# Mask steps, norm scalars and the accumulator's transpose in a four-layer graph network: what goes to VectorE, and in which order

## The chip, the cores and the metric

The kernel runs on one core of a Trainium2 chip. A core has TensorE (PE, matrix products into PSUM), VectorE (DVE), ScalarE (ACT), GpSimd (POOL), SyncE (SP, which issues most DMAs here) and 16 DMA engines. Each engine works through its own queue in order; they wait for one another by semaphores. The metric is the device time of one execution in microseconds. Instructions of the profile are named by line of the kernel before (L557), engine, and what they write and read (e<-s,mask_add).

## The reference

Sixteen graphs of 1024 nodes with 128 features share one 0/1 adjacency matrix. Three attention layers and one last layer are applied in turn:

```
for l in 0..2:                                   # 8 heads of 16
    Q, K, V = x @ Wq, x @ Wk, x @ Wv
    attn = softmax(where(adj == 0, -inf, Q K^T / 4))
    x = layer_norm(x + (attn @ V) @ Wo + bo) * ln1_g + ln1_b
    x = layer_norm(x + relu(x @ W1 + b1) @ W2 + b2) * ln2_g + ln2_b
h = x @ W; e = leaky_relu(h @ a_src [:, None] + h @ a_dst [None, :], 0.2)
y = softmax(where(adj == 0, -inf, e)) @ h + x
out = layer_norm(y) * ln_gamma + ln_beta
layer_norm(z) = (z - mean) * (var + 1e-5) ** -0.5
```

## The kernel before

The fast path treats 48 **blocks**, one for each pair of image and attention layer, in groups of four images: four blocks of layer 0, four of layer 1, four of layer 2. A block has 32 **steps** (2 groups of heads, 2 halves of the queries, 8 tiles of keys); `now[0]` counts the steps of the whole program, and `now[0] % 32` is the step's place in its block. A step (`score_step`, L537 on) computes two score pairs `s` of 128 keys by 1024 (L545), each in one of three PSUM tiles, and makes masked exponentials `e` of them:

- In a **single** step the first pair goes through ScalarE's exponential (L553) and is then multiplied by the 0/1 mask on GpSimd (L554). The second pair gets a large negative number added where the mask forbids it, on VectorE (L557), and ScalarE's exponential afterwards (L569).
- In a **double** step (`BOTH_ON_DVE`, L41) both pairs go through VectorE's addition and ScalarE's exponential after it; GpSimd does nothing. ScalarE has two exponentials in either case. The exponentials behind an addition are issued a pair late, so that ScalarE doesn't stand waiting for VectorE.

Four steps later (`AHEAD`) `av_step` multiplies the values with the exponentials into the one accumulator `acc` (L574). After 8 such products `finish` transposes it on VectorE (`tt`, L585), inverts the sums (L588) and has GpSimd scale it (`A`, L589); this happens at steps 3, 11, 19 and 27 of a block, and the next half's first product may not start before the transpose has read `acc`.

Between the steps `piece()` puts small tasks of other blocks, by tables of due steps (`AT`): the projections of the next block (values at 5 and 7, keys at 9 and 11, queries at 17 and 19, with VectorE's `lo` at L473 or L477), the previous block's output projection at 13 and 15, the first FFN product at 23, 25, 27 and 29, and the second at 31 and 35 (step 3 of the next block). Output projection and second FFN product end in `add_and_stats`: VectorE adds the residual (L420), takes four statistics (L413) and four aggregates (L415), which leave mean and variance in `mv`. `scalars` on GpSimd then negates the mean (L433), adds epsilon to the variance (L434) and raises it to -1/2 (L435); `subtract_scale` applies both (L441). The first norm of a block does this in two halves of four columns, the second in one of eight. When the last layer of an image is due, its tasks (`last_tasks`: edges at L774, `aggregate` at L779 to L792) run between the steps of other images' blocks.

The order on PE, ACT and SP is the order of the code (`manual_schedule`). On DVE and POOL a scheduler sets the order by priority and modelled readiness: `soon()` raises the priority, and `tc.issue_after(ins)` keeps what follows behind `ins` on that engine. `low[n]` is the subtraction of `lo` traced in step n; a mask addition and a transpose of step n + 2 are kept behind it. `behind["dve"]` is the last mask addition traced.

Of the kernel before, what the change touches and what calls it, by code (L numbers as in the profile page):

```python
# [15 lines left out]
OP = mybir.AluOpType  # L16
# [8 lines left out]
EPS = 1e-5  # L25
# [12 lines left out]
STACK_AT = 24  # L38
AT_END = {3: (12, 21, 22, 24, 25, 26, 27, 28, 30, 31), 2: (8, 9, 13, 14, 15, 16, 17, 18, 20, 21)}
AHEAD = 4  # L40
BOTH_ON_DVE = (2, 6, 7, 8, 17, 21, 23, 25, 26, 29, 30)  # L41
TILES = {"w": 8, "x": LANES + 1, "last": 2}
BLOCKED = -57344.0

# [13 lines left out]
def gnn_stack(tc: tile.TileContext, a: dict, out: bass.AP):  # L58


    nc = tc.nc
    with tc.tile_pool(name="flag", bufs=1) as fp:
        flag = fp.tile([1, 1], I32, name="flag")
        fast_path(tc, a, out, flag)
        bad = nc.values_load(flag[0:1, 0:1], min_val=0, max_val=1024)
        with tc.If(bad > 0):
            general_path(tc, a, out)
# [52 lines left out]
def fast_path(ctx: ExitStack, tc: tile.TileContext, a: dict, out: bass.AP, flag):  # L120
    nc = tc.nc
# [13 lines left out]
    def slot(dtype=F32):  # L135

        return psum.tile([P, N], dtype, tag="s", name="s", bufs=3)

    def bank():

        if head[0] or tail[0]:
            return slot()[:, :512]
        return psum.tile([P, 512], F32, tag="t", name="t", bufs=1)

    head, tail = [True], [False]
# [5 lines left out]
    def e_tile():  # L151
        return work.tile([P, J, 512], F32, tag="e", name="e", bufs=5)
# [174 lines left out]
    for i in range(2):  # L327
        t = const.tile([P, NT, H, HD + 1], F32, name=f"v{i}")
# [4 lines left out]
    def soon():  # L333

        return nullcontext() if head[0] else tc.high_priority(offset=SOON)
# [43 lines left out]
    def by_columns(dst, lhsT, rhs, start=True, stop=True):  # L379

        for j in range(0, P, SLOT):
            cols = lhsT[:, j // SLOT, :] if len(lhsT.shape) == 3 else lhsT[:, j:j + SLOT]
            nc.tensor.matmul(dst[j:j + SLOT, :], cols, rhs, start=start, stop=stop)  # L383
# [5 lines left out]
    def v3(ps):  # L389
        return ps.rearrange("p (t d) -> p t d", d=D)  # L390
# [16 lines left out]
        return (x, work.tile([P, NT, 6], F32, tag="st", name="st", bufs=4),  # L407
                work.tile([P, NT, 2], F32, tag="mv", name="mv", bufs=4))

    def stats(n, ts):  # L410
        z, st, mv = n
        for t in range(ts.start, ts.stop):
            nc.vector.bn_stats(st[:, t, :], z[:, t, :])  # L413
        for t in range(ts.start, ts.stop):
            nc.vector.bn_aggr(mv[:, t, :], st[:, t, :])  # L415

    def add_and_stats(n):
        def out(ts, ps):
            with soon():
                nc.vector.tensor_add(n[0][:, ts, :], v3(ps), n[0][:, ts, :])  # L420
            stats(n, ts)
        return out

    def normalise(n, ts):

        scalars(n, ts)
        subtract_scale(n, ts)

    def scalars(n, ts):

        mv = n[2]
        m, v = mv[:, ts, 0], mv[:, ts, 1]
        nc.gpsimd.tensor_scalar(m, m, -1.0, None, op0=OP.mult)  # L433
        nc.gpsimd.tensor_scalar(v, v, EPS, None, op0=OP.add)  # L434
        nc.gpsimd.tensor_tensor(v, v, half_neg[:, ts], OP.pow)  # L435

    def subtract_scale(n, ts):
# [7 lines left out]
        nc.gpsimd.tensor_mul(z, z, rows(gain, n))  # L445
        nc.gpsimd.tensor_add(z, z, rows(bias, n))

    checks = [0]

    def check_range(r):  # L450

        for k, op in enumerate((OP.min, OP.max)):
            nc.vector.tensor_reduce(chk[:, k, checks[0]:checks[0] + 1].bitcast(I32), r.bitcast(I32), AX.X, op)
        checks[0] += 1
# [66 lines left out]
    behind, low = {}, {}  # L521
# [15 lines left out]
    def score_step(step):  # L537
        m, g, qh, kt = step
        e = e_tile()
        q0 = qh * 512  # L540
        for pp in range(2):
            q, k = state["Wq", g, pp], state["Wk", g, pp]
            ps = slot()
            for r in range(2):
                nc.tensor.matmul(ps[:, r * 512:(r + 1) * 512], k[64 * r:64 * r + 64, kt * P:(kt + 1) * P],  # L545
                                 q[64 * r:64 * r + 64, q0:q0 + 512], start=True, stop=True)
            ev = e[:, 2 * pp:2 * pp + 2, :]
            psv = ps.rearrange("p (r q) -> p r q", q=512)
            both = now[0] % (4 * NT) in BOTH_ON_DVE
            on_pool = pp == 0 and not both  # L550
            m = (mask01 if on_pool else mask_add)[:, kt, q0:q0 + 512][:, None, :].to_broadcast([P, 2, 512])
            if on_pool:
                nc.scalar.activation(ev, psv, AF.Exp, scale=HD ** -0.5)  # L553
                behind["pool"] = nc.gpsimd.tensor_mul(ev, ev, m).ins  # L554
            else:
                with tc.issue_after(low[now[0] - 2]) if now[0] - 2 in low and not head[0] else nullcontext():
                    behind["dve"] = nc.vector.tensor_add(ev, psv, m).ins  # L557
                masked.append((2 * step_no[0] + pp + (not both), ev))
        step_no[0] += 1
        exponentials()  # L560
        return e
# [3 lines left out]
    def exponentials(n=None):  # L565

        while masked and (n is not None or masked[0][0] < 2 * step_no[0] - 1):
            _, ev = masked.pop(0)
            nc.scalar.activation(ev, ev, AF.Exp, scale=HD ** -0.5)  # L569
# [7 lines left out]
    def finish(g, qh, acc):  # L577

        def run():
            if g == 0 and qh == 0:  # L580
                state["A"] = work.tile([P, 2, 16, G, HD], F32, tag="A", name="A", bufs=1)
                state["recs"] = work.tile([P, G, 2, 16], F32, tag="recs", name="recs", bufs=2)
            tt = work.tile([P, 16, SLOT], F32, tag="tt", name="tt", bufs=1)
            with soon(), tc.issue_after(low[now[0] - 2]) if now[0] - 2 in low else nullcontext():
                nc.vector.transpose(tt.rearrange("p a b -> p (a b)"), acc)  # L585
            rec = state["recs"][:, g, qh, :]
            with soon():
                nc.vector.reciprocal(rec, tt[:, :, HD])  # L588
                nc.gpsimd.tensor_mul(state["A"][:, qh, :, g, :], tt[:, :, :HD],  # L589
                                     rec[:, :, None].to_broadcast([P, 16, HD]))  # L590
        return run


    def post_tasks(m, quick=False):
# [40 lines left out]
        def normed(ts):  # L635
            def run():
                with tc.issue_after(behind["pool"]):
                    if ts.start == 0:
                        scalars(s["n2"], slice(0, NT))
                    subtract_scale(s["n2"], ts)  # L640
            return run
# [59 lines left out]
    def last_tasks(b):  # L701
        s = {}
# [76 lines left out]
        def aggregate(v):  # L779
            def run():  # L780
                e, ps = s["e", v], bank()
                for t in range(NT):
                    by_columns(ps[:, :D + 1], e[:, t, :], s["hd"][t // 4][:, t % 4, :], start=(t == 0), stop=(t == NT - 1))
                nc.vector.reciprocal(s["col"][:, 3, v:v + 1], ps[:, D:D + 1])
                nc.vector.scalar_tensor_tensor(s["n"][0][:, v, :], ps[:, :D], s["col"][:, 3, v:v + 1],
                                               state["x", b][:, v, :], op0=OP.mult, op1=OP.add)
                stats(s["n"], slice(v, v + 1))
                if v % 4 == 3:
                    with tc.issue_after(behind["pool"]):
                        normalise(s["n"], slice(v - 3, v + 1))  # L790
                if v == NT - 1:
                    check_range(s["col"].rearrange("p c t -> p (c t)"))  # L792
            return run
# [44 lines left out]
    now = [0]  # L838
# [117 lines left out]
    n = 0  # L956
    with tc.manual_schedule(engines={mybir.EngineType.PE, mybir.EngineType.Activation, mybir.EngineType.SP}):
        for m, (b, l) in enumerate(blocks):
# [3 lines left out]
            for at, (g, qh, kt) in enumerate((g, qh, kt) for g, qh in order for kt in range(NT)):  # L962
# [19 lines left out]
                if FIRST <= n < FIRST + 4:  # L982

                    with tc.manual_schedule(engines={mybir.EngineType.DVE}):
                        e = score_step(step)
                        neighbours(4 + n - FIRST)
                        masks(4 + n - FIRST, mask_rows(4 + n - FIRST))
                else:
                    e = score_step(step)
# [253 lines left out]
```

## Time and profile before

| What | Value |
|---|---|
| Median of 3 runs | 3936.28 us (3936.0 to 3938.77) |
| The profiled execution's own time | 3936.96 us |
| Its span, instructions | 3935.1 us, 109752 |
| Busy: PE, DVE, POOL, ACT | 3742.7, 3512.1, 3386.4, 3289.2 us |
| Mean granted TensorE clock | 0.982 |
| Mask additions on DVE (L557) | 2064 of 1209 ns |
| Mask products on POOL (L554) | 1008 of 2026 ns |
| Negation and epsilon on POOL (L433, L434), four columns | 134 each, of 237 and 227 ns |
| The same, eight columns | 45 each, of 252 and 251 ns |

A row of groups reads: line, engine, operation, out<-in, shapes, count | busy us, mean ns of one | idle time of the engine just before them, and what ended it. A row of the timeline reads: start us, length us, engine, line, operation, out<-in, shapes, count, and in brackets the idle time before it with what ended it. Busy time of PE includes matmuls whose modelled end was stretched by a wait, so a busy PE can still have lost time. Two VectorE instructions can overlap by some 0.08 us, so the distance of starts says what one costs.

### The profile page before, as it was taken

The page shows a single profiled execution, that of the slowest core. Times are in us where ns is not written, and L with a number is a line of the kernel's source. Part 1 is how long each engine was busy: PE and PEld are TensorE (multiplying, and loading weights), DVE is VectorE, ACT ScalarE, POOL GpSimd, SP SyncE. Part 2 cuts the span into 40 slices and gives each one's busy share as a digit, 9 for nine tenths or more (in the row PEclk, how much of TensorE's full clock was granted, in tenths as well). Part 3 has the DMA queues.
Part 4 walks back from the last instruction along what each step waited for, and adds up shares of the span by engine and source line. Part 5 has one row for each costly group of instructions (what it writes and reads, how often), then busy time and mean ns, then how long its engine had stood idle before and what let it go on. Part 6 is the DMA issues. An engine that isn't in the chain of part 4 may idle for free.

```text
span 3935.1 us, 109752 instructions
## 1 busy us (share of the span) xinstructions
PE 3742.7 (95%) x44385; PEld 1519.1 (39%) x44385; DVE 3512.1 (89%) x5908; ACT 3289.2 (84%) x3797; POOL 3386.4 (86%) x2923
## 2 busy tenths in 40 slices
PE   7999999999989999999998999999999999999987
PEld 2333333344434333334444433333444433333346
DVE  6999999989989999998998999998898999999876
ACT  7989999977877999997777899998776799999850
POOL 4889999978888999997888999998887899999784
PEclk8999999999999999999999999999999999999998
DMA  5423424322223423332322324333231324324200
GB/s 137 117 69 96 99 71 109 86 66 70 71 66 92 101 71 104 86 86 69 79 71 77 90 68 103 90 79 98 69 88 51 85 68 100 95 73 110 56 8 21
DMA packets 245889, 319.30 MB, mean 81 GB/s; under 512 B 51073, under 2 KB 174209, under 8 KB 245377
## 3 DMA queue, kind: packets, MB, share of 16 engines
q1 hardware_dynamic: 243840, 311.52, 31.3%
q8 instruction: 354, 5.80, 0.6%
q14 instruction: 159, 1.29, 0.1%
q10 hardware_dynamic: 1536, 0.68, 0.1%
HBM read 58.53 MB, written 51.38 MB: 28 GB/s over the span
## 4 chain that ended last, share of the span: by engine, by line
PE 50%; DVE 22%; ACT 11%; issue 6%; POOL 5%; DMA 3%; SPq 3%; DVEq 0%; ACTq 0%; POOLq 0%
PE acc L574 18%; DVE e L557 15%; PE t L383 15%; PE s L545 13%; ACT e L569 5%; ACT e L553 3%; POOL e L554 2%; PE s L769 2%; ACT hT L649 2%; PE s L383 1%; DMA x1T<-tr 1%; DVE st L413 1%; POOL x L441 1%; DVE xb L357 1%; DVE aT L603 1%
## 5 line engine op out<-in xcount | busy, mean ns | idle before, releaser
L557 DVE TENSOR_TENSOR e<-s,mask_add 128x1024 f32<-128x1024 f32 x2064 | 2417.5, 1209 | 136.7 <-PE s L545 99.2
L554 POOL TENSOR_TENSOR e<-e,mask 128x1024 f32<-128x1024 f32 x1008 | 2028.6, 2026 | 387.6 <-ACT e L553 373.8
L569 ACT ACTIVATE e<-e 128x1024 f32<-128x1024 f32 x2064 | 2144.6, 1061 | 176.9 <-DVE e L557 152.2
L574 PE MATMUL acc<-e,v 128*17 128x512 f32 x12288 | 1628.2, 602 | 12.7 <-POOL e L554 9.3
L545 PE MATMUL s<-Wq,Wk 64*128 64x512 f32 x6144 | 1228.6, 461 | 74.6 <-DVE e L557 32.0
L553 ACT ACTIVATE e<-s 128x1024 f32<-128x1024 f32 x1008 | 1031.9, 1024 | 294.1 <-PE s L545 279.5
L545 PEld LDWEIGHTS s<-Wq,Wk 64*128 64x128 f32 x6144 | 503.6, 185 | 1157.5 <-DVE e L557 464.3
L441 POOL TENSOR_SCALAR x<-x,mv 128x128 f32<-128x128 f32 x896 | 388.1, 448 | 19.5
L574 PEld LDWEIGHTS acc<-e,v 128*17 128x17 f32 x12288 | 205.7, 95 | 515.4 <-issue 428.3
L435 POOL TENSOR_TENSOR mv<-mv,half_neg 128x4 f32<-128x4 f32 (+1 forms) x179 | 213.9, 1195 | 14.1
L420 DVE TENSOR_TENSOR x<-t,x 128x512 f32<-128x512 f32 x191 | 131.9, 690 | 100.0 <-PE t L383 96.7
L413 DVE BATCH_NORM_STATS2 st<-x 128x6 f32<-128x128 f32 x896 | 204.6, 282 | 9.0
L774 DVE SCALAR_TENSOR_TENSOR ee<-s,mask 128x256 f32<-128x256 f32 x512 | 179.5, 412 | 32.4 <-PE s L769 32.4
L383 PE MATMUL t<-hd,ee 128*32 128x129 f32 x6656 | 205.7, 274 | 2.7 <-DVE x L420 2.7
L383 PE MATMUL t<-x1T,W 128*32 128x512 f32 x1520 | 199.3, 596 | 4.8 <-issue 2.4
L383 PEld LDWEIGHTS t<-W,hT 128*32 128x32 f32 x6080 | 169.2, 110 | 60.1 <-issue 48.7
L383 PEld LDWEIGHTS t<-hd,ee 128*32 128x32 f32 x6656 | 178.8, 109 | 16.4 <-DVE x L420 5.3
L383 PE MATMUL t<-W,hT 128*32 128x128 f32 x6080 | 183.6, 273 | 0.2
L585 DVE STREAM_TRANSPOSE tt<-acc 128x512 f32<-128x512 f32 x192 | 135.6, 706 | 33.4 <-PE acc L574 33.4
L649 ACT ACTIVATE hT<-t,b 128x512 f32<-128x512 f32 x190 | 130.6, 688 | 4.9 <-PE t L383 4.4
L515 POOL TENSOR_TENSOR x<-x,bo 128x1024 f32<-128x1024 f32 x48 | 114.6, 2388 | 9.2 <-DMA ai<-in_adj_dram 6.7
L589 POOL TENSOR_TENSOR A<-tt,recs 128x256 f32<-128x256 f32 x192 | 119.8, 624 | 0.2 <-DVE recs L588 0.2
(145 smaller groups left out, 2536.5 us busy)
## 6 DMA issues: line engine op xcount, KB each, us to landing
Wk<-hi SPq DMA_DIRECT2D x384, 128.0 KB
Wk<-lo SPq DMA_DIRECT2D x384, 128.0 KB
Wq<-hi SPq DMA_DIRECT2D x384, 128.0 KB
Wq<-lo SPq DMA_DIRECT2D x384, 128.0 KB
tr<-xb SPq DMA_DIRECT2D x656, 64.0 KB
x1T<-tr SPq DMA_DIRECT2D x90, 256.0 KB
xT<-tr SPq DMA_DIRECT2D x74, 256.0 KB
x<-in_x_dram SPq DMA_DIRECT2D x124, 64.0 KB
```

The lines of the kernel that those rows point to most:

```text
L383: nc.tensor.matmul(dst[j:j + SLOT, :], cols, rhs, start=start, stop=stop)
L413: nc.vector.bn_stats(st[:, t, :], z[:, t, :])
L435: nc.gpsimd.tensor_tensor(v, v, half_neg[:, ts], OP.pow)
L441: nc.gpsimd.tensor_scalar(z[:, t, :], z[:, t, :], mv[:, t, 0:1], mv[:, t, 1:2], op0=OP.add, op1=OP.mult)
L545: nc.tensor.matmul(ps[:, r * 512:(r + 1) * 512], k[64 * r:64 * r + 64, kt * P:(kt + 1) * P], q[64 * r:64 * r + 64, q0:q0 + 512], start=Tru ...
L553: nc.scalar.activation(ev, psv, AF.Exp, scale=HD ** -0.5)
L554: behind["pool"] = nc.gpsimd.tensor_mul(ev, ev, m).ins
L557: behind["dve"] = nc.vector.tensor_add(ev, psv, m).ins
L569: nc.scalar.activation(ev, ev, AF.Exp, scale=HD ** -0.5)
L574: nc.tensor.matmul(acc[j * SLOT:j * SLOT + HD + 1, :], v_bufs[m % 2][:, kt, 2 * j + g, :], e[:, j, :], start=first, stop=last)
L649: nc.scalar.activation(s["h", f, h], ps, AF.Relu, bias=w["b1"][:, f:f + 1], scale=1.0)
L774: nc.vector.scalar_tensor_tensor(e[:, :, j * SLOT:(j + 1) * SLOT], ps.rearrange("p (k q) -> p k q", q=P)[:, :, j * SLOT:(j + 1) * SLOT], 1 ...
```

## The change

Three things are done at once. The list of double steps has ten places instead of eleven, six of the old ones gone and five new. The negation and the epsilon become two VectorE instructions directly behind the aggregates (in the last layer behind every fourth), over four columns at a time; GpSimd keeps the power. And two orders on VectorE are set otherwise: a mask addition is kept behind the epsilon of a norm traced in the step before (`summed`), where there is one, else behind `low` as it was; the accumulator's transpose is kept behind the last mask addition instead of behind `low`.

```diff
--- before.py
+++ after.py
@@ -38,7 +38,7 @@
 STACK_AT = 24
 AT_END = {3: (12, 21, 22, 24, 25, 26, 27, 28, 30, 31), 2: (8, 9, 13, 14, 15, 16, 17, 18, 20, 21)}
 AHEAD = 4
-BOTH_ON_DVE = (2, 6, 7, 8, 17, 21, 23, 25, 26, 29, 30)
+BOTH_ON_DVE = (3, 7, 8, 15, 23, 24, 26, 28, 30, 31)
 TILES = {"w": 8, "x": LANES + 1, "last": 2}
 BLOCKED = -57344.0
 
@@ -407,18 +407,24 @@
         return (x, work.tile([P, NT, 6], F32, tag="st", name="st", bufs=4),
                 work.tile([P, NT, 2], F32, tag="mv", name="mv", bufs=4))
 
-    def stats(n, ts):
+    def stats(n, ts, n_last=4):
         z, st, mv = n
         for t in range(ts.start, ts.stop):
             nc.vector.bn_stats(st[:, t, :], z[:, t, :])
         for t in range(ts.start, ts.stop):
-            nc.vector.bn_aggr(mv[:, t, :], st[:, t, :])
+            last = nc.vector.bn_aggr(mv[:, t, :], st[:, t, :])
+        ts = slice(ts.stop - n_last, ts.stop)
+        if n_last:
+            with tc.issue_after(last.ins):
+                nc.vector.tensor_scalar(mv[:, ts, 0], mv[:, ts, 0], -1.0, None, op0=OP.mult)
+                last = nc.vector.tensor_scalar(mv[:, ts, 1], mv[:, ts, 1], EPS, None, op0=OP.add)
+        return last.ins
 
     def add_and_stats(n):
         def out(ts, ps):
             with soon():
                 nc.vector.tensor_add(n[0][:, ts, :], v3(ps), n[0][:, ts, :])
-            stats(n, ts)
+            summed[now[0]] = stats(n, ts)
         return out
 
     def normalise(n, ts):
@@ -428,10 +434,7 @@
 
     def scalars(n, ts):
 
-        mv = n[2]
-        m, v = mv[:, ts, 0], mv[:, ts, 1]
-        nc.gpsimd.tensor_scalar(m, m, -1.0, None, op0=OP.mult)
-        nc.gpsimd.tensor_scalar(v, v, EPS, None, op0=OP.add)
+        v = n[2][:, ts, 1]
         nc.gpsimd.tensor_tensor(v, v, half_neg[:, ts], OP.pow)
 
     def subtract_scale(n, ts):
@@ -445,7 +448,7 @@
         nc.gpsimd.tensor_mul(z, z, rows(gain, n))
         nc.gpsimd.tensor_add(z, z, rows(bias, n))
 
-    checks = [0]
+    checks, summed = [0], {}
 
     def check_range(r):
 
@@ -553,7 +556,8 @@
                 nc.scalar.activation(ev, psv, AF.Exp, scale=HD ** -0.5)
                 behind["pool"] = nc.gpsimd.tensor_mul(ev, ev, m).ins
             else:
-                with tc.issue_after(low[now[0] - 2]) if now[0] - 2 in low and not head[0] else nullcontext():
+                front = summed.get(now[0] - 1, low.get(now[0] - 2))
+                with tc.issue_after(front) if front and not head[0] else nullcontext():
                     behind["dve"] = nc.vector.tensor_add(ev, psv, m).ins
                 masked.append((2 * step_no[0] + pp + (not both), ev))
         step_no[0] += 1
@@ -581,7 +585,7 @@
                 state["A"] = work.tile([P, 2, 16, G, HD], F32, tag="A", name="A", bufs=1)
                 state["recs"] = work.tile([P, G, 2, 16], F32, tag="recs", name="recs", bufs=2)
             tt = work.tile([P, 16, SLOT], F32, tag="tt", name="tt", bufs=1)
-            with soon(), tc.issue_after(low[now[0] - 2]) if now[0] - 2 in low else nullcontext():
+            with soon(), tc.issue_after(behind["dve"]) if not tail[0] else nullcontext():
                 nc.vector.transpose(tt.rearrange("p a b -> p (a b)"), acc)
             rec = state["recs"][:, g, qh, :]
             with soon():
@@ -784,7 +788,7 @@
                 nc.vector.reciprocal(s["col"][:, 3, v:v + 1], ps[:, D:D + 1])
                 nc.vector.scalar_tensor_tensor(s["n"][0][:, v, :], ps[:, :D], s["col"][:, 3, v:v + 1],
                                                state["x", b][:, v, :], op0=OP.mult, op1=OP.add)
-                stats(s["n"], slice(v, v + 1))
+                stats(s["n"], slice(v, v + 1), 4 if v % 4 == 3 else 0)
                 if v % 4 == 3:
                     with tc.issue_after(behind["pool"]):
                         normalise(s["n"], slice(v - 3, v + 1))
```

## Prediction

> **What bounds the kernel now.** I read the page first: the busy shares, the chain that ended last, the costliest groups.
>
> ```profile
> span 3935.1 us, 109752 instructions
> PE 3742.7 (95%) x44385; PEld 1519.1 (39%) x44385; DVE 3512.1 (89%) x5908; ACT 3289.2 (84%) x3797; POOL 3386.4 (86%) x2923
> PE 50%; DVE 22%; ACT 11%; issue 6%; POOL 5%; DMA 3%; SPq 3%; DVEq 0%; ACTq 0%; POOLq 0%
> L557 DVE TENSOR_TENSOR e<-s,mask_add 128x1024 f32<-128x1024 f32 x2064 | 2417.5, 1209 | 136.7 <-PE s L545 99.2
> L554 POOL TENSOR_TENSOR e<-e,mask 128x1024 f32<-128x1024 f32 x1008 | 2028.6, 2026 | 387.6 <-ACT e L553 373.8
> ```
>
> No engine stands alone: TensorE has most of the chain, but VectorE, GpSimd and ScalarE are nearly as full. So I cut the span by the first score matmul of each block. Of the 48 blocks 25 last 70.9 to 71.3 us; twelve, in which the last layer of finished images runs beside attention, take 91 to 99 us, and the other eleven 70.5 to 86 us or end the program. The busy times in the stretches of one short and one long block:
>
> ```profile
> 540.58:611.51 70.93, 69.19 (x708) 24.23 (x704) 66.45 (x99) 66.85 (x74) 65.76 (x55) 1.00 0.37 94
> 1405.00:1496.30 91.30, 89.23 (x852) 29.95 (x848) 86.26 (x120) 87.02 (x98) 86.20 (x66) 1.00 0.39 102
> ```
>
> The columns are length, PE, PEld, DVE, ACT, POOL, clock, DMA share, GB/s. In the short block four engines each have 66 to 69 us of work in 71 us. A step without other work takes 1.64 us on the timeline when nothing waits; a projection adds 0.86, the second FFN product 1.78 twice. That is 32 x 1.64 + 12 x 0.86 + 3.56 = 66.4 us, so TensorE loses 4.5 us per short block, its floor being as low as the other engines' work. In the long block nearly every step stands at its own floor (4.15 us where a weighted sum of the last layer runs); I count 1.5 us lost.
>
> So **it is the order of work inside a block that costs**, not one engine's total. Steps are numbered 0 to 31 within a block. TensorE holds three score tiles, so the scores of step n+1 wait until the mask additions of step n-1 and the ScalarE exponential of step n have read theirs. VectorE around step 11:
>
> ```profile
> 563.43 1.21 DVE L557 TENSOR_TENSOR e<-s,mask_add 128x1024 f32<-128x1024 f32 x1
> 564.57 0.74 DVE L477 SCALAR_TENSOR_TENSOR lo<-t,bqkv,hi 128x512 fp32r<-128x512 f32 x1
> 566.26 0.72 DVE L585 STREAM_TRANSPOSE tt<-acc 128x512 f32<-128x512 f32 x1 [0.95 <-PE acc L574]
> 566.90 1.19 DVE L557 TENSOR_TENSOR e<-s,mask_add 128x1024 f32<-128x1024 f32 x1
> ```
>
> The transpose of the finished accumulator stands ahead of the step's mask addition, and VectorE idles 0.95 us for it although those scores are there. Over the run the view of waits has "DVE tt <- PE acc" at 33.4 us in 37 cases, and TensorE's own waits for mask additions at 32.0 us and for the first exponential at 26.8 us.
>
> **The change, part by part.**
>
> *One double step fewer per block.* A double step has two VectorE additions instead of one, an exponential behind the mask instead of ahead of it, and no GpSimd product. Eleven become ten: VectorE loses 48 x 1.13 us (the additions start 1.13 us apart when back to back) = 54 us of work, 1.13 per block; GpSimd gains 48 x 2.0 = 96 us, 2.0 per block; ScalarE's count stays. No DMA moves with it.
>
> *Negation and epsilon.* The rows:
>
> ```profile
> L433 POOL TENSOR_SCALAR mv<-mv 128x4 f32<-128x4 f32 x134 | 31.8, 237 | 82.8 <-DVE mv L415 69.6 <-DVE ext L1012 3.3
> L434 POOL TENSOR_SCALAR mv<-mv 128x4 f32<-128x4 f32 x134 | 30.4, 227 | 9.0
> L415 DVE BATCH_NORM_AGGREGATE mv<-st 128x2 f32<-128x6 f32 x896 | 92.4, 157 | 2.7
> L588 DVE RECIPROCAL recs<-tt 128x16 f32<-128x16 f32 x192 | 47.8, 249 | 5.2
> ```
>
> GpSimd starts the two operations and the power 0.32 us apart: 0.65 us per norm, three norms per block, 1.95 us. That pays for the added product (2.0). VectorE gets two operations behind each of four statistics per block, a form that this trace does not have there. Lower bound: as closely spaced as aggregates, 0.07 us each, 0.14 a pair; nothing below, since an instruction takes its slot. Upper bound: the reciprocal's 0.25 each, 0.5 a pair. I take 0.27: the first waits for the last aggregate (0.16 long, against the 0.07 after which the mask addition starts today), the second starts 0.1 later and holds the mask addition as long. Four pairs are 1.1 us (0.6 to 2.0), so VectorE's total per block changes by -1.13 + 1.1 = 0 (-0.6 to +0.9). What hides a pair is the lead of three score tiles; where that is used up, the cost falls on TensorE: in step 2, after FFN product, statistics and mask additions have followed one another. There the mask addition of step 0 ends 1.55 us into step 1 today, TensorE wants its tile at 1.64, and with the pair it ends at 1.83: 0.2 us lost.
>
> [...]
>
> *The wait of the mask additions behind the statistics of the step before.* Queued behind such an addition is everything of VectorE, and ScalarE's exponential and the next scores wait for it. But the trace has the statistics ahead of the additions in steps 0, 4, 14 and 16 already (add, four statistics, four aggregates, addition), so only the pair is new.
>
> *The transpose behind the mask additions of its step.* It acts in step 11; at 3, 19 and 27 the additions stand first already. The 0.95 us of idle is filled. What is late next is the exponential: the first one of step 10 ends 0.6 us into step 11, TensorE wants that tile at 0.34, so some of the loss stays. The next accumulation needs the transpose 3.7 us into step 11; it ends at 3.3.
>
> *Placement.* Doubles go from 2, 6, 17, 21, 25, 29 to 3, 15, 24, 28, 31. I followed one short block by these rules from the rows above (addition 1.13 apart and 1.21 long, exponentials 0.95 apart, 2.0 per product).
> - Steps 31 to 3: VectorE idles 1.17 us at the end of step 31 today, so the double there is covered; the double gone from 2 removes 0.27 of loss in step 3, the pair adds 0.2. Together 0.
> - Steps 4 to 13: 22.4 us today, floor 20.9. Without the double at 6 and with the transpose later VectorE is never the last; ScalarE is (12 exponentials, two copies and a cast between the long steps), and 21.5 remain: -0.9.
> - Steps 14 to 17: 8.3, no loss today. The double at 15 lies between two statistics: the first exponential of step 16 is issued behind that of step 15, which waits for VectorE, so it ends 0.7 us into step 17 where TensorE wants the tile at 0.34: +0.5.
> - Steps 18 to 30: 28.1, of it 2.5 lost, mostly for the first exponential of a bare step. In a double step TensorE waits for an addition instead, and 24, 26, 28, 30 are bare: -0.5.
> GpSimd has seven products and two norms in steps 16 to 22; the latest product ends 2 us before its weighted sum wants it.
>
> Sum: -0.9 us per short block, 25 x 0.9 = 22; half as much in nine others, 4; 0.3 in the twelve long ones and the last, 4. **30 us less** on 3936.96 us of the profiled execution (span 3935.1): **3907 us**. That execution lies 0.7 us over the median of 3936.28, which is nothing here.
>
> **The rivals.** The measurement tells 0.2% (8 us) from no change.
> - *Larger gain.* Without the forced waits of ScalarE (I kept 2.5 of its 4.1 us of idle per block) the block falls to 69 us: 25 x 1.9 + 15 = 63 us, 3874. For it: ScalarE's 66.85 us is the floor. Against it: it must wait out the long steps 3 and 31.
> - *Nothing moves.* The eight small operations take back the addition that left, and the remaining waits are ScalarE's: 3937. For it: the sums per engine are equal to 0.1 us.
> - *Slower: the double in step 15.* Two statistics with their pairs (2.05 each) and four additions (4.5) are 8.6 us of VectorE in steps 14 to 16, whose TensorE floor is 5.8; today it is 6.9. If the lead is gone there, the added 1.7 us all fall on TensorE in steps 16 to 19; against the 0.9 + 0.5 gained elsewhere minus another 0.7 where tiles are taken in a worse order (today TensorE waits in steps 11 and 13 for the tile read last but one), +1.0 per short block, 25 + 6 in the rest: 3968. It decides from 1.4 us lost in steps 14 to 19 over today.
> - That the change does not do what it says: the order of VectorE is the scheduler's, and the transpose could stay ahead where the last addition counted is an older one. Then 15 us of gain are left, inside the first case.
>
> **How the numbers follow.** Forecast 0.48 (3880 to 3928), larger gain 0.17 (3850 to 3880), nothing moves 0.10 (3929 to 3944), slower 0.25 (3945 to 3985). Faster: 0.48 + 0.17 = 0.65. The range leaves out the outer part of both ends, a tenth each, and holds the pair's bounds (25 blocks by -0.5 to +0.9 us are -13 to +22 us): 3860 to 3972.
>
> **What would show it.** Right: 2016 additions and 1056 products; in short blocks no VectorE idle ahead of the transpose in step 11; the pair 0.2 to 0.3 us; short blocks of 70 us; TensorE's waits for additions under 25 us. Wrong: a pair of 0.5 us, ScalarE idle over 1 us in steps 15 to 18, TensorE waits that grow in steps 16 to 19, or products that come late to their weighted sums in steps 20 to 24.

## The result and the profile after

The changed kernel takes 4188.14 us (median of 4 runs, 4186.56 to 4192.55) against 3936.77 us: ratio 1.0638 (95% interval 1.0623 to 1.0653). It is **6.4% slower**, 251 us, where 30 us less were forecast. The page of the changed kernel, whose lines are shifted: the mask addition is L561, the product L557, the exponential behind the mask L573, the pair L419 and L420, the power L438.

```profile
span 4185.5 us, 109797 instructions
PE 3806.2 (91%) x44385; PEld 1534.0 (37%) x44385; DVE 3825.9 (91%) x6308; ACT 3283.5 (78%) x3797; POOL 3392.8 (81%) x2613
L557 POOL TENSOR_TENSOR e<-e,mask 128x1024 f32<-128x1024 f32 x1056 | 2121.1, 2026 | 538.3 <-ACT e L556 531.8
L561 DVE TENSOR_TENSOR e<-s,mask_add 128x1024 f32<-128x1024 f32 x2016 | 2370.5, 1212 | 150.8 <-PE s L548 127.2
L573 ACT ACTIVATE e<-e 128x1024 f32<-128x1024 f32 x2016 | 2091.8, 1066 | 443.2 <-DVE e L561 426.5
L548 PE MATMUL s<-Wq,Wk 64*128 64x512 f32 x6144 | 1252.0, 470 | 253.4 <-DVE e L561 209.5
L419 DVE TENSOR_SCALAR mv<-mv 128x4 f32<-128x4 f32 x224 | 348.4, 1555 | 7.0
```

VectorE has 314 us more of busy time although it lost 48 additions; the last row holds it, **224 negations of four numbers per partition at 1555 ns each in the mean**. Every other engine became less full. TensorE's own waits for mask additions rose from 32.0 to 209.5 us, ScalarE's from 152.2 to 426.5. A short block lasts 75.7 us instead of 70.9. The mean granted TensorE clock fell from 0.982 to 0.970, but that is not the cause: a short block whose whole stretch has a clock of 1.00 lasts 70.93 us before (540.58 to 611.51) and 75.75 us after (559.55 to 635.30).

The answers for the two lines of the pair, in a group by form and, for the first, by shortest, median and longest:

```profile
L420 DVE TENSOR_SCALAR mv<-mv 128x4 f32<-128x4 f32 x224 | 41.3, 184 | 0.0
L419 DVE TENSOR_SCALAR mv<-mv x224: 109/1622/6106, 138.3 to 4172.7; 128x4 f32<-128x4 f32 x112
```

The same operation over the same four columns takes 0.11 or 6.1 us. VectorE and GpSimd in the timeline around one pair (step 15 of a short block):

```profile
594.51 0.36 DVE L415 BATCH_NORM_AGGREGATE mv<-st 128x2 f32<-128x6 f32 x4
594.91 2.04 DVE L419 TENSOR_SCALAR mv<-mv 128x4 f32<-128x4 f32 x1
596.86 0.15 DVE L420 TENSOR_SCALAR mv<-mv 128x4 f32<-128x4 f32 x1
596.93 3.47 DVE L561 TENSOR_TENSOR e<-s,mask_add 128x1024 f32<-128x1024 f32 x3
```

```profile
590.93 5.99 POOL L557 TENSOR_TENSOR e<-e,mask 128x1024 f32<-128x1024 f32 x3
597.09 1.01 POOL L438 TENSOR_TENSOR mv<-mv,half_neg 128x4 f32<-128x4 f32 x1 [0.18 <-DVE mv L420]
```

Three products end at 596.92 and the negation at 596.95. Over the run 195 of the 224 last more than 0.25 us, and each of these ends 23 to 32 ns after a GpSimd instruction ended, 187 times a mask product. The others take 0.11 to 0.19 us, nearly all 0.17. The trace shows no semaphore wait for it: **the negation stands in VectorE while GpSimd works**. In 37 cases, all in steps 14 and 15, more than one GpSimd instruction ends under it. Where GpSimd's next instruction follows at once, VectorE got in between at 77 such joints and was passed over at 48; what decides it the runs do not show. The second operation mostly follows through the same gap, 0.15 us.

### The profile page after: what moved, and what is told of

Read it like the earlier page. It is cut to its first block, busy times and chain, and to the rows that moved or that the text cites. A ratio compares the mean times of both kernels' runs of the same rounds, so it can differ in the third digit from the quotient of the medians.

```text
span 4185.5 us, 109797 instructions
## 1 busy us (share of the span) xinstructions
PE 3806.2 (91%) x44385; PEld 1534.0 (37%) x44385; DVE 3825.9 (91%) x6308; ACT 3283.5 (78%) x3797; POOL 3392.8 (81%) x2613
## 5 line engine op out<-in xcount | busy, mean ns | idle before, releaser
L557 POOL TENSOR_TENSOR e<-e,mask 128x1024 f32<-128x1024 f32 x1056 | 2121.1, 2026 | 538.3 <-ACT e L556 531.8
L561 DVE TENSOR_TENSOR e<-s,mask_add 128x1024 f32<-128x1024 f32 x2016 | 2370.5, 1212 | 150.8 <-PE s L548 127.2
L573 ACT ACTIVATE e<-e 128x1024 f32<-128x1024 f32 x2016 | 2091.8, 1066 | 443.2 <-DVE e L561 426.5
L578 PE MATMUL acc<-e,v 128*17 128x512 f32 x12288 | 1657.0, 612 | 7.9 <-DVE tt L589 7.5
L548 PE MATMUL s<-Wq,Wk 64*128 64x512 f32 x6144 | 1252.0, 470 | 253.4 <-DVE e L561 209.5
L556 ACT ACTIVATE e<-s 128x1024 f32<-128x1024 f32 x1056 | 1082.3, 1025 | 270.9 <-PE s L548 267.7
L548 PEld LDWEIGHTS s<-Wq,Wk 64*128 64x128 f32 x6144 | 514.3, 188 | 1369.4 <-DVE e L561 586.5
L419 DVE TENSOR_SCALAR mv<-mv 128x4 f32<-128x4 f32 x224 | 348.4, 1555 | 7.0
L438 POOL TENSOR_TENSOR mv<-mv,half_neg 128x4 f32<-128x4 f32 (+1 forms) x179 | 209.7, 1171 | 88.0 <-DVE mv L420 84.0
```

Source lines behind the costliest of these rows:

```text
L419: nc.vector.tensor_scalar(mv[:, ts, 0], mv[:, ts, 0], -1.0, None, op0=OP.mult)
L578: nc.tensor.matmul(acc[j * SLOT:j * SLOT + HD + 1, :], v_bufs[m % 2][:, kt, 2 * j + g, :], e[:, j, :], start=first, stop=last)
```

## The experiments

Three theories were put up after the result: A, the pair waits for GpSimd's instructions; B, the new places of the double steps cost the time; C, such an operation is slow by itself. Each run is compared with the kernel before on the same chip (medians 3937.9 to 3939.4 us).

**The placement alone** (against the changed kernel)

```diff
-    def stats(n, ts, n_last=4):
+    def stats(n, ts, n_last=0):
...
-        v = n[2][:, ts, 1]
+        mv = n[2]
+        m, v = mv[:, ts, 0], mv[:, ts, 1]
+        nc.gpsimd.tensor_scalar(m, m, -1.0, None, op0=OP.mult)
+        nc.gpsimd.tensor_scalar(v, v, EPS, None, op0=OP.add)
...
```

> The changed kernel's ten double steps and its orders on VectorE, but negation and epsilon back on GpSimd ahead of the power as in the kernel before. Three theories stand. A: the first operation of the pair on VectorE cannot run while GpSimd executes an instruction (in the changed kernel it lasts 1555 ns in the mean and ends about 25 ns after a GpSimd instruction does), and this costs nearly all of the 250 us. B: the new places of the double steps cost it, above all the one between two statistics. C: an operation of this kind and size is slow on VectorE by itself, whatever GpSimd does. A and C: 3895 to 3945 us, the time that the prediction gave to the placement. B: above 4150 us.

3922.85 us, ratio 0.9959 (0.9945 to 0.9973). B falls: list and orders alone gain 16 us. In the view of TensorE's waits of this run stands where it lost time instead:

```profile
PE acc L581 <- POOL e L560: 67.4, 162, 2.5
PE s L551 <- DVE e L564: 22.0, 51, 1.0
```

Waits for mask additions fell from 32.0 to 22.0 us, but the products now come late to their weighted sums (9.3 us in 12 cases before).

**The pair alone** (against the kernel before)

```diff
+        if n_last:
+            with tc.issue_after(last.ins):
+                nc.vector.tensor_scalar(mv[:, ts, 0], mv[:, ts, 0], -1.0, None, op0=OP.mult)
+                nc.vector.tensor_scalar(mv[:, ts, 1], mv[:, ts, 1], EPS, None, op0=OP.add)
...
-        nc.gpsimd.tensor_scalar(m, m, -1.0, None, op0=OP.mult)
-        nc.gpsimd.tensor_scalar(v, v, EPS, None, op0=OP.add)
...
```

> The kernel before, with its eleven double steps and its orders, and only negation and epsilon moved to VectorE behind the aggregates. A and C: 4130 to 4230 us, the pair's first operation again 1.3 to 1.7 us in the mean. B: 3930 to 3960 us.

4070.36 us, ratio 1.0332 (1.0315 to 1.0349): 131 us, under the expected span, and the first operation is 0.81 us in the mean. The pair costs by itself, but only half of what is lost in the changed kernel. Something in the placement doubles it; two runs below ask what.

**The pair by single columns** (against the changed kernel)

```diff
-                nc.vector.tensor_scalar(mv[:, ts, 0], mv[:, ts, 0], -1.0, None, op0=OP.mult)
-                last = nc.vector.tensor_scalar(mv[:, ts, 1], mv[:, ts, 1], EPS, None, op0=OP.add)
+                for t in range(ts.start, ts.stop):
+                    nc.vector.tensor_scalar(mv[:, t, 0:1], mv[:, t, 0:1], -1.0, None, op0=OP.mult)
+                for t in range(ts.start, ts.stop):
+                    last = nc.vector.tensor_scalar(mv[:, t, 1:2], mv[:, t, 1:2], EPS, None, op0=OP.add)
```

> The changed kernel, but the pair is done one column at a time: eight VectorE operations of one element per partition behind each four statistics instead of two of four elements. A, if it is the form over several columns alone that must wait for GpSimd: 0.07 to 0.17 us each, none of them stretched to GpSimd's end, and 3920 to 3990 us. A, if every operation of this kind must wait: the first of eight is as long as now, 4190 to 4260 us. C: eight slow operations, several times 250 us more than the kernel before, above 5000 us. B: as the changed kernel, 4150 to 4230 us.

3920.46 us, ratio 0.9952 (0.9936 to 0.9969). The same arithmetic, on the same engine, at the same place, in **four times as many instructions, is 268 us faster** than the pair. By form:

```profile
L422 DVE TENSOR_SCALAR mv<-mv 128x1 f32<-128x1 f32 x896 | 73.0, 144 | 0.0
L420 DVE TENSOR_SCALAR mv<-mv 128x1 f32<-128x1 f32 x896 | 67.9, 138 | 0.0
```

The longest of the 1792 takes 154 ns, though 1514 of them begin and end within one GpSimd instruction. C falls, and A holds for the form over several columns alone.

**GpSimd's products in halves** (against the changed kernel)

```diff
-                behind["pool"] = nc.gpsimd.tensor_mul(ev, ev, m).ins
+                for r in range(2):
+                    behind["pool"] = nc.gpsimd.tensor_mul(ev[:, r], ev[:, r], m[:, r]).ins
```

> The changed kernel with each GpSimd mask product cut into two of half the size. A: the first operation waits for the rest of a GpSimd instruction half as long; its mean falls from 1.56 to 0.7 to 1.0 us, and the time by some 80 to 130 us, to 4060 to 4110 us, unless instructions of GpSimd that follow at once keep VectorE out for longer, then both stay where they are. C: the mean stays at 1.5 to 1.6 us. B: the time stays within 20 us of 4188, and the wait plays no part in it.

4134.41 us (ratio 1.0494, 1.0476 to 1.0511); a half product takes 1.11 us.

```profile
L419 DVE TENSOR_SCALAR mv<-mv x224: 106/704/7090, 136.5 to 4126.2; 128x4 f32<-128x4 f32 x112
```

The median wait halves with the instruction it waits for (1622 to 704 ns), as A has it. The mean falls only to 1152, less than expected, and the time by 54 us instead of 80 to 130: in 41 cases VectorE sat through several halves, and for the pairs that run in step 15 the mean rose from 2.69 to 3.56 us. GpSimd's 2121 us of products also became 2270.

**The pair as operations of two tensors** (against the changed kernel)

```diff
...
-                nc.vector.tensor_scalar(mv[:, ts, 0], mv[:, ts, 0], -1.0, None, op0=OP.mult)
-                last = nc.vector.tensor_scalar(mv[:, ts, 1], mv[:, ts, 1], EPS, None, op0=OP.add)
+                nc.vector.tensor_tensor(mv[:, ts, 0], mv[:, ts, 0], minus[:, :n_last], OP.mult)
+                last = nc.vector.tensor_tensor(mv[:, ts, 1], mv[:, ts, 1], small[:, :n_last], OP.add)
```

> The changed kernel with the pair as operations of two tensors: the mean times a tile of -1, the variance plus a tile of epsilon, over four columns each. What has to wait for GpSimd is told apart: if any operation over several columns that reads its operands from SBUF alone must, or one with two SBUF inputs, the first lasts 1.3 to 1.7 us in the mean and the time is 4170 to 4210 us. If only the form with one tensor and a constant must, both last 0.1 to 0.3 us and the time is 3910 to 3930 us.

4190.53 us (ratio 1.064, 1.0621 to 1.0659), no better than the changed kernel:

```profile
L422 DVE TENSOR_TENSOR mv<-mv,minus 128x4 f32<-128x4 f32 x224 | 341.8, 1526 | 7.0
```

So an operation with two SBUF inputs waits in the same way. Two common operations of VectorE do not: a mask addition, which has one input in PSUM, took 1.21 us in the mean and at most 1.23 us before and after the change, and `bn_stats`, which reads 128 columns of one SBUF tensor, 0.28 us in the mean and at most 0.30. Of the three forms tried for the negation, the two over four columns wait, with a constant (1.56 us in the mean) and with a second tensor (1.53 us), and the one over a single column does not (0.14 us). The runs show which forms wait, and for what; why these and not the others they do not show.

**Which part of the placement doubles it.** In the changed kernel the mask additions of the next step stand behind the pair; with the pair alone the scheduler had put one between aggregates and pair in 166 of the 224 places. First, the changed kernel with the additions kept behind the aggregates only:

```diff
-                last = nc.vector.tensor_scalar(mv[:, ts, 1], mv[:, ts, 1], EPS, None, op0=OP.add)
+                nc.vector.tensor_scalar(mv[:, ts, 1], mv[:, ts, 1], EPS, None, op0=OP.add)
```

> The changed kernel, but the mask additions of the next step are kept behind the aggregates and no longer behind the pair, which lets the scheduler put one addition between aggregates and pair, as it stands in the run with the pair alone (4070). Theory: the wait for GpSimd costs twice, by its length and by the mask additions that stand behind it. If the order is what makes 131 us with the old list and orders into 265 with the new ones: 4040 to 4090 us, the pair's first operation 0.7 to 1.0 us in the mean. If the ten new double steps do it, because GpSimd then runs two products in a row beside the pair: 4150 to 4190 us.

4028.63 us (ratio 1.0234, 1.0214 to 1.0253): **160 of the 251 us hang on the order of pair and addition.** The first operation is 0.89 us in the mean instead of 1.56, as the addition that goes first covers part of GpSimd's product, and that addition no longer stands still. How much each of the two brings, the run does not tell apart. The other way round, the run with the pair alone, and the additions kept behind it:

```diff
...
+                front = summed.get(now[0] - 1, low.get(now[0] - 2))
+                with tc.issue_after(front) if front and not head[0] else nullcontext():
...
```

> The run with the pair alone (the old list, the old order of the transpose; 4070), with the mask additions of the next step kept behind the pair as in the changed kernel. If the order makes the difference: 4150 to 4210 us and a first operation of 1.3 to 1.7 us in the mean. If the list does: 4060 to 4090 us.

4281.95 us (ratio 1.0878, 1.086 to 1.0896), more than expected and the slowest of all, with a first operation of 1.31 us in the mean: the order adds 212 us with the old list too. The list is no culprit: it gains in both pairs of runs, 42 us with the additions ahead (4070 to 4029) and 94 with them behind (4282 to 4188), each time together with the transpose's order.

**The two parts of the placement alone** (against the kernel before): first the transpose's order, then the list.

```diff
-            with soon(), tc.issue_after(low[now[0] - 2]) if now[0] - 2 in low else nullcontext():
+            with soon(), tc.issue_after(behind["dve"]) if not tail[0] else nullcontext():
...
-BOTH_ON_DVE = (2, 6, 7, 8, 17, 21, 23, 25, 26, 29, 30)
+BOTH_ON_DVE = (3, 7, 8, 15, 23, 24, 26, 28, 30, 31)
```

> The kernel before with one line changed: the accumulator's transpose is kept behind the last mask addition of its step, as in the changed kernel. By the prediction's step on the transpose the 33.4 us that VectorE waits ahead of it go, and a short block falls by 0.3 to 0.6 us: 3920 to 3930 us. If the loss at that place belongs to ScalarE's exponential anyway: 3934 to 3940 us.

> The kernel before with the ten new double steps alone; orders and negation and epsilon as before. By the prediction's steps on placement a short block gains 0.3 to 0.6 us and the double between two statistics takes 0.5 of it back: 3920 to 3935 us. If GpSimd, with 48 products more, is late for the weighted sums (TensorE waited 67.4 us for its products where the new list ran with negation and epsilon on GpSimd): 3935 to 3960 us.

The order: 3931.26 us, ratio 0.9981 (0.9972 to 0.9991), a little under the expected gain; VectorE's 33.4 us ahead of the transpose no longer stand in the waits, and a short block lasts 70.6 us. The list: 3924.57 us, ratio 0.9967 (0.9954 to 0.998), 70.5 us. Its gain is as forecast, but TensorE waits 59.7 us for products.

**Epsilon by columns, no negation** (against the run by single columns)

```diff
-                for t in range(ts.start, ts.stop):
-                    nc.vector.tensor_scalar(mv[:, t, 0:1], mv[:, t, 0:1], -1.0, None, op0=OP.mult)
...
-            nc.gpsimd.tensor_scalar(z[:, t, :], z[:, t, :], mv[:, t, 0:1], mv[:, t, 1:2], op0=OP.add, op1=OP.mult)
+            nc.gpsimd.tensor_scalar(z[:, t, :], z[:, t, :], mv[:, t, 0:1], mv[:, t, 1:2], op0=OP.subtract, op1=OP.mult)
```

> The changed kernel without the negation (GpSimd subtracts the mean instead of adding its negative) and with epsilon added one column at a time on VectorE, four operations behind each four statistics. Theory A: no operation waits for GpSimd, 0.3 us of VectorE go per four statistics against the run with eight single columns (3920), of which some comes back where VectorE is late: 3905 to 3918 us, under both kernels. If the rest of that run's loss is ScalarE's or GpSimd's: 3917 to 3923 us.

4070.64 us (1.0339, 1.0325 to 1.0353), far off, and it says nothing of its question: GpSimd's subtraction with product takes 795 ns where addition with product takes 448.

```profile
L444 POOL TENSOR_SCALAR x<-x,mv 128x128 f32<-128x128 f32 x896 | 698.8, 795 | 17.1
```

**Only the negation by columns.** If GpSimd is late in the placement and VectorE has room for four short operations, the pair can be shared. Against the run by single columns, epsilon goes back to GpSimd:

```diff
-                    nc.vector.tensor_scalar(mv[:, t, 0:1], mv[:, t, 0:1], -1.0, None, op0=OP.mult)
-                for t in range(ts.start, ts.stop):
-                    last = nc.vector.tensor_scalar(mv[:, t, 1:2], mv[:, t, 1:2], EPS, None, op0=OP.add)
+                    last = nc.vector.tensor_scalar(mv[:, t, 0:1], mv[:, t, 0:1], -1.0, None, op0=OP.mult)
...
+        nc.gpsimd.tensor_scalar(v, v, EPS, None, op0=OP.add)
         nc.gpsimd.tensor_tensor(v, v, half_neg[:, ts], OP.pow)
```

> The changed kernel with the negation on VectorE, one column at a time (four operations of one element per partition), and epsilon on GpSimd ahead of the power. No VectorE operation waits for GpSimd. VectorE has 0.28 us less per four statistics than in the run with eight columns (3920), GpSimd 0.32 us more per norm, and less than with both on GpSimd (3923): 3910 to 3920 us, the fastest of all, if the two engines' shares decide; 3919 to 3924 us if the waits lie elsewhere.

**3895.75 us, ratio 0.9894 (0.9877 to 0.991): faster than both kernels**, 42 us under the one before, and beyond what was expected. A short block lasts 69.7 us. TensorE's waits:

```profile
PE s L549 <- DVE e L562: 23.9, 54, 1.5
PE acc L579 <- POOL e L558: 19.4, 25, 2.0
PE t L345 <- DMA x<-in_x_dram: 18.5, 3, 6.2
PE s L549 <- ACT e L557: 14.0, 44, 0.4
```

The late products are down from 67.4 to 19.4 us without the mask additions getting later (22.0 to 23.9). Last, the same on the kernel before, with its list and orders:

```diff
...
+                for t in range(ts.start, ts.stop):
+                    nc.vector.tensor_scalar(mv[:, t, 0:1], mv[:, t, 0:1], -1.0, None, op0=OP.mult)
...
-        nc.gpsimd.tensor_scalar(m, m, -1.0, None, op0=OP.mult)
...
```

> The kernel before (its eleven double steps and its orders) with the negation on VectorE one column at a time, epsilon and power on GpSimd. It tells how much of the 42 us of the fastest version belongs to the negation's new place alone. If the new list pays only together with it (GpSimd relieved, and then a product more): 3925 to 3940 us here. If the negation's place does it alone: 3895 to 3915 us.

3955.59 us, ratio 1.0048 (1.0034 to 1.0061): slower, beyond the expected span. Relieving GpSimd at VectorE's cost paid here only with the list and orders that take an addition from VectorE (3895.75 us).

## Why the prediction was wrong

- **The step that failed is the price of the pair.** It was bounded between 0.07 us each, by the aggregates' spacing, and 0.25 us each, by the reciprocal, 0.27 us was taken for the two, and no rival let it cost more than 0.5. Measured in the mean: 1.56 us for the first operation, up to 6.1, and 0.18 for the second. The upper bound came from other operations, though the trace of before held the same kind, a `tensor_scalar` from SBUF to SBUF, in its rare groups of the weights' setup:

```profile
L304 DVE TENSOR_SCALAR Wq<-Wq,ln_gc 128x128 f32<-128x128 f32 x2 | 2.3, 1150 | 0.0
L304 DVE TENSOR_SCALAR Wk<-Wk,ln_gc 128x128 f32<-128x128 f32 x2 | 0.5, 274 | 0.0
```

  The same work took 1150 and 274 ns in the mean. Of the two on `Wq` one took 275 ns; the other began at 219.05, while GpSimd's products ran from 216.95 to 220.99, and ended at 221.07. A group of one shape whose mean is four times that of its twin was the warning. Its 2.02 us would have been a better bound, though the longest negation passed it too.
- **The wait of the additions behind the pair was called nothing new**, since the statistics stood ahead already. True of the order, wrong as a cost: whatever stands behind a wait of unknown length takes that length over. The run with the additions ahead is 160 of the 251 us faster.
- **What hides a pair** was right in its mechanism: the lead of three score tiles is nearly used up in step 1. It does not cover the 1.7 us that the first operation takes there; TensorE lost 1.66 us at the start of step 2, the place that the prediction named:

```profile
564.57 0.73 PE L548 MATMUL s<-Wq,Wk 64*128 64x512 f32 x4 [1.66 <-DVE e L561]
```

- **The rival that was slower** named the right place for a wrong reason. From the first score matmul of step 14 to that of step 20 the 25 short blocks take 13.3 us in the mean before and 16.7 in the changed kernel, 3.4 of the 4.8 us that such a block lost. But the double between two statistics costs nothing there without the pair: 13.2 us with the placement alone. In the changed kernel the pair in step 15 is the longest, 2.69 us in the mean, and 31 of the 37 cases in which more than one GpSimd instruction ends under it lie there.
- **The transpose's order**: VectorE's idle went as foretold. TensorE's waits for the first exponential stayed (26.8 us before, 27.1 in that run), and step 11 lasts 3.19 us as before. The 0.3 us per short block were gained in step 13 instead (3.04 to 2.70 us).
- **The placement**: forecast -0.9 us per short block and 30 us, with the cost of a pair in it; measured -0.4 and 16 us with no pair on VectorE. By stretches, counted in the same way as above: -0.1 in steps 31 to 3 (forecast 0), -0.7 in 4 to 13 (-0.9), +0.3 in 14 to 17 (+0.5), but 0.0 instead of -0.5 in 18 to 30. The wrong step is that the latest product ends 2 us before its weighted sum wants it: 67.4 us of waits. With GpSimd relieved of the negation the short block does fall by 1.2 us.
- **The sums per engine** (VectorE 0, GpSimd +2.0 - 1.95 per block) counted durations right for GpSimd: 3386.4 to 3392.8 us of busy time. They could not see that one engine's instruction takes the other's time: 348.4 us of VectorE for 224 negations.

## What to carry to other kernels

Before a small operation is moved to VectorE, look at what GpSimd does at that moment and at the form of the operation: a `tensor_scalar` over four columns from SBUF to SBUF mostly stood still here until GpSimd's instruction ended (195 of 224 negations, 1.56 us in the mean), and an operation of two SBUF tensors took as long (1.53 us). The one-column form of the same arithmetic did not (0.14 us, at most 0.154), and four instructions beat one (3920 us against 4188). Price a form that a trace hardly has by the spread of that form's own rare rows, not by the mean of other operations, and keep nothing urgent behind an instruction whose length another engine sets.

## What the runs showed of the hardware

- VectorE's negation of four SBUF columns (0.15 to 0.17 us where GpSimd is idle) ended 23 to 32 ns after a GpSimd instruction in all 195 cases of the changed kernel in which it lasted over 0.25 us; GpSimd instructions that followed one another at once kept it out for several of them (6.1 us), but not always (it got in at 77 such joints and was passed over at 48). Nor is it always held: in the run with the pair alone, 31 negations that began 5 to 106 ns after a GpSimd `tensor_scalar` of 0.45 us ended within it, none longer than 0.20 us.
- Single columns were not stretched in the run by single columns: 1792 operations, at most 154 ns, 1514 of them within one GpSimd instruction.
- GpSimd's `tensor_scalar` over 128 columns took 448 ns in the mean as addition and product, 795 as subtraction and product; negating the mean beforehand is what bought the faster form here.
